# The end of a fused attention and feed-forward kernel: the last tile's operands turned by TensorE, products and results moved to GpSimd and ScalarE

## The chip, the cores and the metric

The kernel runs on one core of one Trainium2 chip. The metric is the device time of one execution in microseconds (us). Engines: TensorE (PE, with its weight load PEld), VectorE (DVE), ScalarE (ACT), GpSimd (POOL) and SyncE (SP), which only issues DMAs. Each engine works through its own instructions in the order in which the kernel writes them.

## The reference

`x` is 64 x 64 x 1024 in float32, 4096 tokens of 1024 numbers. The reference is

```
x = x + attn(cond(x))           # a 64x64 product per batch row, 32 heads, output projection
x = x + ffn(cond2(x))           # cond2: base product, plus a routed low-rank term
```

Only the second line's last part matters here. For a tile of 128 tokens, `z = cond2(x)` is rounded to bfloat16, and then

```
def dynamic_quant(x, inv):                       # per token
    xs = x * inv
    scale = max(max(abs(xs)) / 127, 1e-8)
    return clip(round(xs / scale), -127, 127), scale

qg, sg = dynamic_quant(z, inv_gate);  qu, su = dynamic_quant(z, inv_up)
gate = (qg @ w_gate.T) * sg * s_wgate            # 1024 -> 512
up   = (qu @ w_up.T)   * su * s_wup
inter = bfloat16(clip(silu(gate) * up, -10, 10))
qi, si = dynamic_quant(inter, inv_inter)         # 512 wide
out = x + (qi @ w_down.T) * si * s_wdown         # 512 -> 1024
```

## The kernel before

Tokens come in 32 tiles of 128, worked in 16 pairs. Attention fills the first two thirds of the time, then the output projection, then `second_stage`. There a software pipeline holds three pairs at once: a pair's router and base products run while the pair before it is in its quantized products and the one before that in its `down` products. The order of all steps is written out by hand (`manual_schedule`): first a loop over pairs, then a straight list of calls for the last three. In that list `p` is the last pair, `q` the one before it, `r` the one before that; (q, 1) below means tile 1 of pair q. So the order of the calls is the order on each engine, and a call that issues work on several engines takes a place in each of their queues.

The steps of one tile, with the names of their tiles and the lines of the profile:

- `rounded` (L1497): ScalarE rounds the base product out of PSUM to `z`.
- `quant_a` (L1531, L1535): VectorE multiplies `z` (or `inter`) by the inverse smoothing row into `q_g`, `q_u` or `q_i`, and takes the largest absolute value `am`. `quant_half` (L1546, L1547) and `quant_whole` (L1553) do the same by halves of 512 for the last tile, (p, 1), as its second half of `z` comes late.
- `scaled_down`: VectorE makes the scale `sc` (L1559) and its reciprocal `rs` (L1561), and ScalarE rounds in two activations (L1562, L1564) to `qb` in bfloat16.
- `quant_b`: VectorE clips `qb` (L1572), and the tile is transposed to `qT`, by a DMA from SP (L1575), or, with `by_pe`, by TensorE into PSUM (L1579, tile `qTp`) and a ScalarE copy (L1580). Only the `i` operands of the last pair go by TensorE.
- `gate_or_up` (L1589): eight matmuls give `pg` or `pu` in PSUM.
- `scaled` (L1594, L1600): VectorE scales into `og` or `ou` by a scalar_tensor_tensor (STT below); ScalarE takes the sigmoid `e` of `og`.
- `glu` (L1606, L1607, L1609): VectorE makes `inter`. It goes through `quant_a` and `quant_b` as `i`.
- `down` (L1619): two halves of four matmuls each give `pd` in PSUM.
- `result`: VectorE scales `pd` into `y` (L1628). For most tiles GpSimd then issues a DMA that adds `y` to the output in memory (L1636). For (q, 1) and the last pair, `x` is already on the chip (`x_l`, `x_ll`): GpSimd or VectorE adds it (L1632), and SP stores each half (L1633).

Tiles of the pool `p2` have two buffers for each tag, those of `p1p` one; a new tile waits until the old one in its buffer has no reader left, and a DMA that reads it counts. The tag of `y` is

```
y = p2.tile([P, H], F32, tag="q" if p == NPAIR - 1 else "y", name=f"y_{p}_{t}")
```

so that `y` of the last pair uses the buffers of `q_g` and `q_u`. Small products, and those of the last tile, share eight PSUM banks in two pools of four.

Of the kernel before, what the change touches and what calls it, by code (L numbers as in the profile page):

```python
# [11 lines left out]
F32 = mybir.dt.float32  # L12
# [3 lines left out]
AF = mybir.ActivationFunctionType  # L16
ALU = mybir.AluOpType
AX = mybir.AxisListType
PSUM = bass.MemoryType.PSUM

P = 128
# [1264 lines left out]
def second_stage(tc, a, out_t, xT_d, ident, ps_g, KC, NT, H, C, half, comb, op):  # L1286


    nc = tc.nc
# [7 lines left out]
    hs = [slice(0, HH), slice(HH, H)]  # L1297

    with ExitStack() as ctx:
# [7 lines left out]
        def load_row(name, src, n, pool=None):  # L1307
            t = (pool or w).tile([P, n], F32, tag=name, name=name)
            nc.sync.dma_start(t, bcast_rows(src))
            return t  # L1310
# [35 lines left out]
        p2 = ctx.enter_context(tc.tile_pool(name="q3", bufs=2, reuse_waits="tile"))  # L1346
# [3 lines left out]
        st = st1  # L1350
# [12 lines left out]
        sd_w = load_row("sd_w", a["s_wdown"], H)  # L1363
# [131 lines left out]
        def rounded(p, t, n):  # L1495
            s = st[p]
            nc.scalar.copy(s["z"][:, t, hs[n]], s.pop(("ps", t, n)))  # L1497
# [22 lines left out]
            elif i == 3:  # L1520
                nc.vector.tensor_tensor(z[:, 1, hs[0]], ps, s.pop("u2"), ALU.add)

        def quant_a(p, t, nm, between=None):

            s = st[p]
            src, inv, n = {
                "g": (lambda: s["z"][:, t, :], ig, H), "u": (lambda: s["z"][:, t, :], iu, H),
                "i": (lambda: s.pop(("inter", t)), ii, I),
            }[nm]
            q = p2.tile([P, n], F32, tag="q" + ("i" if nm == "i" else ""), name=f"q_{nm}_{p}_{t}")  # L1530
            nc.vector.tensor_tensor(q, src(), inv, ALU.mult)  # L1531
            if between:
                quant_b(*between)
            am = sm.tile([P, 1], F32, tag="am" + nm, name=f"am_{nm}_{p}_{t}")
            nc.vector.tensor_reduce(am, q, AX.X, ALU.max, apply_absolute_value=True)  # L1535
            scaled_down(p, t, nm, q, am, n)

        def quant_half(p, t, nm, n):

            s = st[p]  # L1540
            inv = ig if nm == "g" else iu
            if n == 0:
                s["q", nm] = p2.tile([P, H], F32, tag="q", name=f"q_{nm}_{p}_{t}")
                s["am", nm] = sm.tile([P, 2], F32, tag="amh" + nm, name=f"amh_{nm}_{p}_{t}")
            q = s["q", nm][:, hs[n]]
            nc.vector.tensor_tensor(q, s["z"][:, t, hs[n]], inv[:, hs[n]], ALU.mult)  # L1546
            nc.vector.tensor_reduce(s["am", nm][:, n:n + 1], q, AX.X, ALU.max, apply_absolute_value=True)  # L1547

        def quant_whole(p, t, nm):
            s = st[p]  # L1550
            q, am2 = s.pop(("q", nm)), s.pop(("am", nm))
            am = sm.tile([P, 1], F32, tag="am" + nm, name=f"am_{nm}_{p}_{t}")
            nc.vector.tensor_tensor(am, am2[:, 0:1], am2[:, 1:2], ALU.max)  # L1553
            scaled_down(p, t, nm, q, am, H)

        def scaled_down(p, t, nm, q, am, n):
            s = st[p]
            sc = s["sc", nm, t] = sm.tile([P, 1], F32, tag="sc" + nm, name=f"sc_{nm}_{p}_{t}", bufs=4)
            nc.vector.tensor_scalar(sc, am, 1.0 / QMAX, 1e-8, ALU.mult, ALU.max)  # L1559
            rs = sm.tile([P, 1], F32, tag="rs" + nm, name=f"rs_{nm}_{p}_{t}")  # L1560
            nc.vector.reciprocal(rs, sc)  # L1561
            nc.scalar.activation(q, q, AF.Copy, bias=MAGIC, scale=rs)  # L1562
            qb = s["qb", nm, t] = p2.tile([P, n], BF16, tag="qb" + nm, name=f"qb_{nm}_{p}_{t}")
            nc.scalar.activation(qb, q, AF.Copy, bias=-MAGIC)  # L1564

        def quant_b(p, t, nm, by_pe=False):


            s = st[p]
            n = I if nm == "i" else H  # L1570
            qb = s.pop(("qb", nm, t))
            nc.vector.tensor_scalar(qb, qb, QMAX, -QMAX, ALU.min, ALU.max)  # L1572
            s["qT", nm, t] = qT = p2.tile([P, n // P, P], BF16, tag="qT" + nm, name=f"qT_{nm}_{p}_{t}")
            if not by_pe:
                nc.sync.dma_start(qT, qb, transpose=True)  # L1575
                return
            ps = ps_g.tile([P, n // P, P], BF16, tag="g", name=f"qTp_{nm}_{p}_{t}")
            for c in range(n // P):
                nc.tensor.transpose(ps[:, c, :], qb[:, c * P:(c + 1) * P], ident_b)  # L1579
            nc.scalar.copy(qT, ps)  # L1580

        def gate_or_up(p, t, nm):
            s = st[p]
            qT = s.pop(("qT", nm, t))

            pool, tag = (ps_g, "g") if (p, t) == (NPAIR - 1, 1) else (ps_h, "h")
            ps = s["pgu", nm, t] = pool.tile([P, I], F32, tag=tag, name=f"p{nm}_{p}_{t}")
            for k in range(KC):
                nc.tensor.matmul(ps, qT[:, k, :], wt_b["w" + nm][:, k, :], start=(k == 0), stop=(k == KC - 1))  # L1589

        def scaled(p, t, nm):
            s = st[p]
            o = p1p.tile([P, I], F32, tag="o" + nm, name=f"o{nm}_{p}_{t}")
            nc.vector.scalar_tensor_tensor(  # L1594
                o, s.pop(("pgu", nm, t)), s.pop(("sc", nm, t)), sg_w if nm == "g" else su_w, ALU.mult, ALU.mult
            )
            s["o", nm, t] = o
            if nm == "g":
                e = p1p.tile([P, I], F32, tag="e", name=f"e_{p}_{t}")
                nc.scalar.activation(e, o, AF.Sigmoid)  # L1600
                s["e", t] = e

        def glu(p, t):
            s = st[p]
            e, g, u = s.pop(("e", t)), s.pop(("o", "g", t)), s.pop(("o", "u", t))
            nc.vector.tensor_mul(e, g, e)  # L1606
            nc.vector.tensor_mul(e, e, u)  # L1607
            inter = p1p.tile([P, I], BF16, tag="inter", name=f"inter_{p}_{t}")
            nc.vector.tensor_scalar(inter, e, LIMIT, -LIMIT, ALU.min, ALU.max)  # L1609
            s["inter", t] = inter  # L1610

        def down(p, t):
            s = st[p]
            qT = s.pop(("qT", "i", t))
            for n in range(2):
                pool, tag = (ps_g, "g") if p == NPAIR - 1 else (ps_h, "h")
                ps = s["pd", t, n] = pool.tile([P, HH], F32, tag=tag, name=f"pd_{p}_{t}_{n}")
                for k in range(IC):
                    nc.tensor.matmul(  # L1619
                        ps, qT[:, k, :], wt_b["wd"][:, k, hs[n]], start=(k == 0), stop=(k == IC - 1)  # L1620
                    )

        def result(p, t, *adds):
            s = st[p]
            y = p2.tile([P, H], F32, tag="q" if p == NPAIR - 1 else "y", name=f"y_{p}_{t}")
            si = s.pop(("sc", "i", t))
            for n in range(2):
                nc.vector.scalar_tensor_tensor(  # L1628
                    y[:, hs[n]], s.pop(("pd", t, n)), si, sd_w[:, hs[n]], ALU.mult, ALU.mult
                )  # L1630
                if adds:
                    adds[n % len(adds)].tensor_add(y[:, hs[n]], y[:, hs[n]], s["x", t][:, hs[n]])  # L1632
                    nc.sync.dma_start(out_t[2 * p + t, :, hs[n]], y[:, hs[n]])  # L1633
            if not adds:

                nc.gpsimd.dma_start(out_t[2 * p + t], y, accum_op=ALU.add)  # L1636

        def do(when, f, *args):
# [5 lines left out]
        for p in range(NPAIR - 1):  # L1644
            q, r = p - 1, p - 2
# [53 lines left out]
        p, q, r = NPAIR - 1, NPAIR - 2, NPAIR - 3  # L1699
# [14 lines left out]
        route(p)  # L1714
        quant_b(r, 1, "i")
        result(r, 0)
        quant_a(q, 0, "u")
        down(r, 1)
# [25 lines left out]
        glu(q, 1)  # L1744
        gate_or_up(p, 0, "g")
        rounded(p, 1, 1)
        quant_half(p, 1, "g", 0)
        quant_half(p, 1, "u", 0)
        gate_or_up(p, 0, "u")
        quant_half(p, 1, "g", 1)  # L1750
        quant_whole(p, 1, "g")
        quant_b(q, 0, "i")
        quant_half(p, 1, "u", 1)
        quant_whole(p, 1, "u")
        down(q, 0)
        quant_b(p, 1, "g")
        quant_a(q, 1, "i")
        scaled(p, 0, "g")
        scaled(p, 0, "u")
        quant_b(p, 1, "u")  # L1760
        gate_or_up(p, 1, "g")
        glu(p, 0)
        quant_b(q, 1, "i")
        gate_or_up(p, 1, "u")
        quant_a(p, 0, "i")
        scaled(p, 1, "g")
        scaled(p, 1, "u")
        down(q, 1)
        quant_b(p, 0, "i", True)
        glu(p, 1)  # L1770
        quant_a(p, 1, "i")
        result(q, 0)
        down(p, 0)
        quant_b(p, 1, "i", True)
        result(q, 1, nc.gpsimd)
        result(p, 0, nc.gpsimd, nc.vector)
        down(p, 1)
        result(p, 1, nc.vector)

# [53 lines left out]
```

## Time and profile before

| | before |
|---|---|
| median of 3 runs | 2405.47 us (2402.76 to 2409.4) |
| the profiled execution's own time | 2406.19 us |
| its span, first to last instruction | 2404.4 us |
| mean granted TensorE clock | 0.997 |
| TensorE busy | 2367.6 us (98%) |
| VectorE busy | 1334.5 us (56%) |
| ScalarE busy | 936.2 us (39%) |
| GpSimd busy | 418.7 us (17%) |
| last matmul of a base product (pb) starts | 2369.9 us |
| last instruction of VectorE ends | 2397.7 us |

All times inside the span count from its start. In the profile's rows a group is named by line, engine, operation, output and inputs, shape and count; a bracket gives the engine's idle time before it and what ended that. A wait is put down to the semaphore that came last. A busy TensorE is not TensorE at its peak, since matmuls overlap. In the windows each engine has its busy time and number of instructions, then the granted clock, the DMA engines' share and the rate.

### The profile page before, as it was taken

How to read it: one execution, taken by the hardware profiler on the slowest of the kernel's cores; microseconds unless marked ns; L12 is line 12 of the kernel's file. 1: busy time of each engine (PE TensorE's matmuls, PEld its weight loads, DVE VectorE, ACT ScalarE, POOL GpSimd, SP SyncE). 2: the span in 40 equal slices, each digit the busy share in tenths (PEclk: the TensorE clock that was granted, in tenths of full speed). 3: DMA queues.
4: the chain of work that ended last, by engine and by line, in shares of the span. 5: the costliest groups of instructions: out<-in, count | busy, mean ns of one | idle time of the engine just before them, and what ended most of it. 6: DMA issues, size and time to landing. Idle time of an engine off the chain costs nothing.

```text
span 2404.4 us, 41907 instructions
## 1 busy us (share of the span) xinstructions
PE 2367.6 (98%) x17066; PEld 1628.5 (68%) x17104; DVE 1334.5 (56%) x2584; ACT 936.2 (39%) x1220; POOL 418.7 (17%) x470
## 2 busy tenths in 40 slices
PE   8999999999999999999999999999999999999997
PEld 7888888888888888888888444444454545454452
DVE  3573474464543644633535533324377878777787
ACT  1344344343344443443434544343333333333333
POOL 4121112111122223220000333334100000000000
PEclk9999999999999999999999999999999999999999
DMA  7899799899899998997967788877733443444353
GB/s 229 217 240 248 190 228 241 221 232 220 208 232 274 212 255 230 242 237 179 207 188 196 213 257 258 275 218 248 239 77 75 90 79 83 84 86 82 70 119 76
DMA packets 612395, 453.84 MB, mean 189 GB/s; under 512 B 362465, under 2 KB 524258, under 8 KB 606690
## 3 DMA queue, kind: packets, MB, share of 16 engines
q1 hardware_dynamic: 581522, 393.91, 63.2%
q0 software_dynamic: 12240, 40.38, 7.9%
q10 hardware_dynamic: 18432, 16.79, 3.1%
q8 instruction: 137, 2.24, 0.4%
q14 instruction: 64, 0.52, 0.1%
HBM read 274.02 MB, written 91.23 MB: 152 GB/s over the span
## 4 chain that ended last, share of the span: by engine, by line
PE 92%; DMA 2%; DVE 1%; SPq 1%; issue 1%; ACT 0%; ACTq 0%; DVEq 0%
PE poa L1129 5%; PE poc L1129 5%; PE pod L1129 5%; PE psvc L530 4%; PE psva L530 4%; PE psvd L530 4%; PE pbc L1129 4%; PE pbd L1129 4%; PE pba L1129 4%; PE pskc L509 4%; PE pskd L509 4%; PE pska L509 4%; PE psqa L509 4%; PE psqd L509 4%; PE psqc L509 4%; PE pr L1398 2%
## 5 line engine op out<-in xcount | busy, mean ns | idle before, releaser
L582 ACT ACTIVATE prob<-prob 128x512 f32<-128x512 f32 x128 | 80.6, 629 | 346.7 <-DVE prob L578 338.6
L608 ACT COPY pT<-phT 128x1024 int16<-128x1024 int16 x128 | 165.4, 1339 | 25.4 <-DMA phT<-ph 21.4
L596 ACT COPY ph<-prob 128x1024 int16<-128x1024 int16 x128 | 133.5, 1043 | 63.1 <-DVE prob L590 38.4
L442 POOL COPY yB<-yhT 128x512 int16<-128x512 int16 (+1 forms) x84 | 75.8, 955 | 426.4 <-DMA yhT<-yh 426.4
L1636 POOL DMA_DIRECT2D out_dram<-y x29 | 25.2, 869 | 656.2 <-DVE y L1628 644.4
L577 DVE TENSOR_REDUCE mx<-s 128x8 f32<-128x512 f32 x128 | 87.4, 682 | 71.6 <-PE s L568 71.6
L1250 POOL TENSOR_TENSOR xo<-xo,ob 128x1024 f32<-128x1024 f32 x32 | 83.5, 2629 | 228.2 <-DVE prob L578 189.5
L509 PE MATMUL psqa<-yB,wq 128*128 128x256 f32 x512 | 121.1, 379 | 0.5 <-ACT psqp L479 0.5
L509 PE MATMUL pska<-yB,wk 128*128 128x256 f32 x512 | 120.9, 379 | 0.0
L1224 ACT COPY xh<-xo 128x1024 int16<-128x1024 int16 x64 | 64.4, 1041 | 142.8 <-DVE xo L1269 142.8
L530 PE MATMUL psva<-wv,yB 128*128 128x256 f32 x512 | 115.8, 379 | 0.0
L1129 PE MATMUL poa<-woA,cx 128*128 128x512 f32 x256 | 115.3, 593 | 0.0
L1129 PE MATMUL pba<-wtA,x1T 128*128 128x512 f32 x240 | 107.9, 592 | 0.0
L1235 ACT COPY xTo<-xhT 128x1024 int16<-128x1024 int16 x64 | 84.7, 1337 | 58.4 <-DMA xhT<-xh 53.3
L530 PEld LDWEIGHTS psva<-wv,yB 128*128 128x128 f32 x512 | 97.2, 190 | 14.0 <-issue 0.8
L509 PEld LDWEIGHTS psqa<-yB,wq 128*128 128x128 f32 x512 | 97.1, 190 | 14.0 <-ACT psqp L479 0.9
L509 PEld LDWEIGHTS pska<-yB,wk 128*128 128x128 f32 x512 | 97.3, 190 | 13.2
L633 ACT ACTIVATE co<-banks,bqkv 128x256 f32<-128x256 f32 x128 | 60.7, 474 | 109.3 <-PE banks L411 79.8
L1266 POOL TENSOR_TENSOR xo<-xo,ou 128x512 f32<-128x512 f32 x48 | 59.9, 1275 | 191.8 <-DVE ou L1263 191.8
L590 DVE TENSOR_TENSOR prob<-prob,den 128x512 f32<-128x512 f32 x128 | 89.4, 699 | 4.4
L578 DVE TENSOR_TENSOR prob<-s,mx 128x512 f32<-128x512 f32 x128 | 88.5, 691 | 4.5
L1129 PEld LDWEIGHTS poa<-woA,cx 128*128 128x128 f32 x256 | 48.5, 190 | 60.0 <-issue 59.5
(255 smaller groups left out, 4945.8 us busy)
## 6 DMA issues: line engine op xcount, KB each, us to landing
wv<-v_d SPq DMA_DIRECT2D x56, 512.0 KB
wq<-q_d SPq DMA_DIRECT2D x28, 1024.0 KB
wk<-k_d SPq DMA_DIRECT2D x28, 1024.0 KB
wq<-in_qkvw_dram SPq DMA_DIRECT2D x100, 256.0 KB
wk<-in_qkvw_dram SPq DMA_DIRECT2D x100, 256.0 KB
wv<-in_qkvw_dram SPq DMA_DIRECT2D x50, 512.0 KB
x<-in_x_dram SPq DMA_DIRECT2D x32, 512.0 KB
ctx_d<-co ACTq DMA_DIRECT2D x128, 128.0 KB
```

The costliest lines, as they stand in the source:

```text
L442: nc.gpsimd.tensor_copy(dst, src[:, :, :, halves[r] if hf else r])
L509: nc.tensor.matmul(ps[:, 0:HB], A[:, SLOT[A_OF[i]], k, :], B[B_OF[i]][:, k, :], start=first and k == 0, stop=k == KQ - 1, skip_group_check ...
L530: nc.tensor.matmul(ps[:, j * VC:(j + 1) * VC], B[B_OF[i]][:, k, j * P:(j + 1) * P], A[:, k, :], start=first and j == 0 and k == 0, stop=k ...
L577: nc.vector.tensor_reduce(mx, ps[:, :, n, :, :], AX.X, ALU.max)
L578: nc.vector.tensor_tensor(p.rearrange("p j h k -> p h j k"), ps[:, :, n, :, :], mx.unsqueeze(3).to_broadcast([P, HPC, 2, C]), ALU.subtract,)
L582: nc.scalar.activation(p, p, AF.Exp, scale=scale)
L590: nc.vector.tensor_tensor(p, p, den.unsqueeze(2).to_broadcast([P, n, C]), ALU.mult)
L596: nc.scalar.copy(h, planes(p.rearrange("p n k -> p (n k)")))
L608: nc.scalar.copy(planes(pT.rearrange("p a b q -> p (a b q)")), hT)
L1129: self.nc.tensor.matmul(ps, self.B[self.B_OF[i]][:, k, :], self.A[self.A_OF[i]][:, k, :], start=first and k == 0, stop=k == self.KQ - 1, s ...
L1235: nc.scalar.copy(planes(xT.rearrange("p k q -> p (k q)")), hT)
L1250: nc.gpsimd.tensor_add(s["x"][:, t, :], s["x"][:, t, :], self.ob)
```

## The change

It is made in the helpers of the end and in the order of the last calls.

- `quant_b` has no yes or no any more but takes the function that copies the transposed operand out of PSUM. The gate operand of (p, 1) is turned by TensorE and copied by VectorE, its up operand turned by TensorE and copied by ScalarE; before, DMAs turned both.
- `quant_a` and `quant_half` take the engine of the product. GpSimd does the second half of `q_u` of (p, 1), and `q_i` of (q, 1) and of (p, 0). The maximum of a half is a step of its own (`half_maximum`).
- `result_by_act` does the results of pair q: ScalarE scales `pd` by the token's scale, GpSimd multiplies by the row `sd_w`, and for (q, 1) GpSimd also adds `x`. Its `y` has the tag `q`.
- The order: the clip and DMA of `qb_i` of (q, 0) come after both scales of (p, 1); `result` of (q, 0) moves up ahead of `glu(p, 0)`; `result` of (p, 0) moves ahead of the last tile's `quant_b`.

```diff
-        def quant_half(p, t, nm, n):
+        def quant_half(p, t, nm, n, eng=nc.vector):
...
-            nc.vector.tensor_tensor(q, s["z"][:, t, hs[n]], inv[:, hs[n]], ALU.mult)
-            nc.vector.tensor_reduce(s["am", nm][:, n:n + 1], q, AX.X, ALU.max, apply_absolute_value=True)
+            eng.tensor_tensor(q, s["z"][:, t, hs[n]], inv[:, hs[n]], ALU.mult)
+            s["am2", nm, n] = lambda: nc.vector.tensor_reduce(
+                s["am", nm][:, n:n + 1], q, AX.X, ALU.max, apply_absolute_value=True
+            )
+
+        def half_maximum(p, nm, n):
+            st[p].pop(("am2", nm, n))()
...
-        def quant_b(p, t, nm, by_pe=False):
+        def quant_b(p, t, nm, by_pe=None):
...
-            nc.scalar.copy(qT, ps)
+            by_pe(qT, ps)
...
+        def result_by_act(p, t, add):
+
+            s = st[p]
+            y = p2.tile([P, H], F32, tag="q", name=f"y_{p}_{t}")
+            si = s.pop(("sc", "i", t))
+            for n in range(2):
+                nc.scalar.activation(y[:, hs[n]], s.pop(("pd", t, n)), AF.Copy, scale=si)
+                nc.gpsimd.tensor_tensor(y[:, hs[n]], y[:, hs[n]], sd_w[:, hs[n]], ALU.mult)
+                if add:
+                    nc.gpsimd.tensor_add(y[:, hs[n]], y[:, hs[n]], s["x", t][:, hs[n]])
+                    nc.sync.dma_start(out_t[2 * p + t, :, hs[n]], y[:, hs[n]])
+            if not add:
+                nc.gpsimd.dma_start(out_t[2 * p + t], y, accum_op=ALU.add)
...
-        quant_half(p, 1, "g", 0)
-        quant_half(p, 1, "u", 0)
+        for nm in ("g", "u"):
+            quant_half(p, 1, nm, 0)
+            half_maximum(p, nm, 0)
         gate_or_up(p, 0, "u")
+        quant_half(p, 1, "u", 1, nc.gpsimd)
         quant_half(p, 1, "g", 1)
+        half_maximum(p, "g", 1)
         quant_whole(p, 1, "g")
+        half_maximum(p, "u", 1)
+        quant_whole(p, 1, "u")
         quant_b(q, 0, "i")
-        quant_half(p, 1, "u", 1)
-        quant_whole(p, 1, "u")
+        quant_a(q, 1, "i", None, nc.gpsimd)
         down(q, 0)
-        quant_b(p, 1, "g")
-        quant_a(q, 1, "i")
         scaled(p, 0, "g")
+        quant_b(p, 1, "g", nc.vector.tensor_copy)
         scaled(p, 0, "u")
-        quant_b(p, 1, "u")
+        quant_b(p, 1, "u", nc.scalar.copy)
         gate_or_up(p, 1, "g")
+        result_by_act(q, 0, False)
+        quant_b(q, 1, "i")
         glu(p, 0)
-        quant_b(q, 1, "i")
         gate_or_up(p, 1, "u")
-        quant_a(p, 0, "i")
+        quant_a(p, 0, "i", None, nc.gpsimd)
         scaled(p, 1, "g")
         scaled(p, 1, "u")
         down(q, 1)
-        quant_b(p, 0, "i", True)
         glu(p, 1)
+        quant_b(p, 0, "i", nc.scalar.copy)
+        result_by_act(q, 1, True)
         quant_a(p, 1, "i")
-        result(q, 0)
         down(p, 0)
-        quant_b(p, 1, "i", True)
-        result(q, 1, nc.gpsimd)
         result(p, 0, nc.gpsimd, nc.vector)
+        quant_b(p, 1, "i", nc.scalar.copy)
         down(p, 1)
         result(p, 1, nc.vector)
```

More of the change, by code (lines that the diff above doesn't have):

```diff
@@ L1521, in after, with quant_a @@
                 nc.vector.tensor_tensor(z[:, 1, hs[0]], ps, s.pop("u2"), ALU.add)
-        def quant_a(p, t, nm, between=None):
+        def quant_a(p, t, nm, between=None, eng=nc.vector):
             s = st[p]
@@ L1530, in quant_a @@
             q = p2.tile([P, n], F32, tag="q" + ("i" if nm == "i" else ""), name=f"q_{nm}_{p}_{t}")
-            nc.vector.tensor_tensor(q, src(), inv, ALU.mult)
+            eng.tensor_tensor(q, src(), inv, ALU.mult)
             if between:
```

## The prediction

> **What bounds the kernel now.** I read the page first, then the windows of the end, the chain of waits there, the timeline of the last 30 us, and last the rows that price what is new.
>
> ```profile
> PE 2367.6 (98%) x17066; PEld 1628.5 (68%) x17104; DVE 1334.5 (56%) x2584; ACT 936.2 (39%) x1220; POOL 418.7 (17%) x470
> ```
> ```profile
> core 0: us, PE busy (x) PEld busy (x) DVE busy (x) ACT busy (x) POOL busy (x), PEclk, DMA share, GB/s
> 2328.00:2371.00 43.00, 42.84 (x132) 19.72 (x134) 32.84 (x71) 17.62 (x23) 1.72 (x2) 1.00 0.42 89
> 2371.00:2383.00 12.00, 7.29 (x33) 2.84 (x32) 10.77 (x25) 6.33 (x8) 0.00 (x0) 1.00 0.30 56
> 2383.00:2405.00 22.00, 8.29 (x38) 3.28 (x37) 13.78 (x24) 4.40 (x7) 5.03 (x4) 0.72 0.40 105
> ```
>
> TensorE is full up to 2371 us and nothing ahead of that is edited, so the change lives in the last 33 us. There VectorE is the busy engine (10.77 of 12 us), GpSimd is empty until 2390. The chain of waits (start, us, what):
>
> ```profile
> 2375.49 0.43 DVE qb_g L1572
> ...
> 2379.33 3.12 DMA qT_u<-qb_u
> 2382.46 0.05 issue
> 2382.50 1.92 PE pu L1589 x8
> ...
> 2390.72 2.73 DVE y L1628 x4
> ...
> 2397.02 0.69 DVE y L1632
> ```
>
> The end is a row of small steps of the last tile (p,1), one transposing DMA of 3.1 us on it, and, after its last clip at 2390.51, VectorE works off eight result steps until 2397.71. From there to the span's end, 6.7 us of stores and closing work are left as they are.
>
> Now the prices. The timeline, and one line's instructions with GpSimd beside it (To) and without (T):
>
> ```profile
> 2390.66 0.86 POOL L1636 DMA_DIRECT2D out_dram<-y  x1 [41.66 <-DVE y L1628]
> 2391.61 2.50 POOL L1632 TENSOR_TENSOR y<-y,x_l 128x512 f32<-128x512 f32 x2
> 2393.48 1.18 DVE L1632 TENSOR_TENSOR y<-y,x_ll 128x512 f32<-128x512 f32 x1
> 2394.07 1.71 POOL L1632 TENSOR_TENSOR y<-y,x_ll 128x512 f32<-128x512 f32 x1
> ```
> ```profile
> L1142 DVE TENSOR_TENSOR To<-cx,To x16: 678/2832/2839, 1325.0 to 1680.8; 128x512 f32<-128x512 f32 x16
> L1142 DVE TENSOR_TENSOR T<-x1T,T x15: 680/683/687, 1716.0 to 2288.0; 128x512 f32<-128x512 f32 x15
> ```
>
> A 512-wide product costs GpSimd 1.26 us against VectorE's 0.69, a store issued by GpSimd holds its queue for 0.86, and GpSimd runs strictly one after the other. A VectorE step with two operands in SBUF that meets a GpSimd product waits until that ends (1.18; 2.83 for 0.68), and GpSimd waits likewise (1.71, ending 1.12 after VectorE's). Steps that read PSUM (L1628, 0.68 each at 2390.72) do not wait. The clock, by windows:
>
> ```profile
> 658.75:662.16 3.41, 1.25 (x6) 1.16 (x7) 0.29 (x1) 3.38 (x4) 0.00 (x0) 1.00 0.79 168
> 662.20:665.50 3.30, 3.30 (x10) 2.59 (x9) 1.89 (x4) 0.32 (x1) 2.15 (x5) 0.50 1.16 312
> 2389.30:2392.70 3.40, 1.16 (x8) 0.63 (x9) 3.25 (x7) 1.73 (x3) 1.95 (x2) 1.00 0.33 23
> 2392.70:2397.70 5.00, 2.11 (x6) 0.46 (x3) 4.90 (x7) 0.00 (x0) 3.08 (x3) 0.50 0.91 245
> ```
>
> Stretches of 3.4 us with TensorE 37% and 34% busy are followed by half the clock.
>
> **The change part by part.** I lay the new written order on each engine with the durations above; between engines 0.04 us pass, 0.14 into GpSimd, and VectorE's next step starts 0.03 after the last one's end if it needs it, 0.08 before it if not, all as the timeline of before shows.
>
> *The second half of q_u to GpSimd, clip of (q,0) moved back.* [...] The clip of qb_i(q,0) stood right behind rs_g (2373.10); now the u maximum (0.69) and am, sc, rs (0.19 each, 0.2 of waiting for GpSimd's q_i(q,1)) go first: 2374.55 to 2374.84. Its DMA needs 2.46 as before (2373.40 to 2375.86), so down(q,0) starts at 2377.33, not 2375.86.
>
> *The last tile's operands turned by TensorE.* Removed: two DMAs of 3.1 us each and their two issues (1.23 each) on SP, which holds nothing else up. Added: eight transposes (row of qTp_i: four in 0.40, 0.056 apart, so 0.61) and a copy of 1024 out of PSUM each. ScalarE copies 1024 16-bit elements out of PSUM in 1.01 (L420). VectorE's copy has no row: 0.42 (the 1024 clip) to 1.23 (the 1024 product); I take 1.22, as for one element a step. By itself a turn of about 1.75 for 3.1. But the transposes of qb_g stand behind down(q,0) on TensorE: 2377.33 + 8 x 0.216 = 2379.06, though qb_g is clipped at 2376.83. They end at 2379.67, and VectorE, whose next instruction is the copy, stands idle for 2.9 us with ou, the u clip, the clip of (q,1) and glu(p,0) queued behind it. Copy to 2380.92, ou 0.74 and clip 0.42 to 2381.92, u transposes to 2382.59, ScalarE's copy to 2383.64. The DMA delivered u at 2382.50: the 1.3 us that a turn saves are gone.
>
> *The results of (q,0) and the product of (p,0).* ScalarE's first half of y (0.59, the PSUM copy, to 0.72, the scaled activation; 0.68 taken) follows that copy: 2384.23. Then GpSimd's queue: 0.14, two products 2.49 (2386.86), the store's issue 0.14 + 0.86 (2387.86), and only then q_i(p,0), to 2389.09. VectorE had that product at 2382.27. Nothing covers the difference: VectorE's next instruction is the maximum of that product, and og, ou and glu of (p,1) queue behind it, though pg is there at 2384.3. **+6.8 us.** Products with a bf16 operand have no GpSimd row: 0.61 (its cast) to 1.71; 1.26 taken.
>
> *From there to rs of (p,1).* Maximum, sc, rs 1.11 (2390.20); og, ou to 2391.51; sigmoid behind ScalarE's q_i, qb_i to 2392.15; glu 1.91 (2394.06); clip of (p,0), product, maximum, sc, rs to 2395.97. That is 6.9 us against 6.8 in before (2382.27 to 2389.06): no change.
>
> *The last steps.* Taken off VectorE: four result steps of 0.68, 2.7 us. But result(p,0) is moved ahead of the last clip and waits for down(p,0), which starts at 2395.70 and, after 6 us without work for TensorE, at half clock (0.43 a matmul, as at 2392.9) ends at 2399.35: STT 2400.13, add 2400.85 (at full clock 2.1 less for the STT, 1.6 for the add, which then meets GpSimd). ScalarE's y(q,1) delays q_i(p,1) by 0.7, hidden by that. Clip of (p,1): 2401.05, up to 1.1 more beside a GpSimd product (no row shows a clip there: 0 to 1.26). Transposes, copy and down at half clock, with that 1.1: the halves lie ready near 2405.5 and 2407.2. There is a new wait too: y of q now uses the buffers named q, so y(p,1) may be written only when y(q,1) is stored. GpSimd's four steps on it (2396.37 plus 4 x 1.26, 0.3 and 0.2 of waits) end at 2401.97; a store from SP needs 0 to 5.5 (the accumulating store's landing), and I take 3.4, since traffic goes on that long after the last issue at 2398.27: 2405.4. Then 0.74 + 0.69 + 0.74 + 0.69: the last add ends at 2408.2 (full clock) to 2408.7, against 2397.71. From rs of (p,1) that is 12.2 to 12.7 us against 8.65 in before (2389.06 to 2397.71), +3.6 to +4.1. **Sum:** 6.8 + 0.1 + 4.1 = **+11.0**, taken at half clock, which the idle stretch ahead is nearest to; +10.5 at full clock.
>
> *The clock.* TensorE waits 3.3 us in one piece (2374.0 to 2377.33), less busy over most cuts into 3.4 us than the two stretches that were halved. Then down(q,0) takes up to 1.73 more, on the path: 0 to +1.75. [...]
>
> [...]
>
> **The rivals.** *TensorE's turning is what counts (faster).* Place: VectorE's queue. It is rid of three products and four result steps (2.7 us), the chain of the DMA in it (3.1 for 1.75). Price: -2.7 and -1.3, near 2401.5. Point: it decides if q_i(p,0) leaves GpSimd by 2382.3, so ScalarE's first half of y by 2377.4, when down(q,0) has just begun. For: GpSimd is empty there in before. Against: the written order.
> *GpSimd's queue does not bind (within 0.3%).* Should q_i(p,0) not have to wait for y(q,0) and its store, it is done near 2385.3 (inter at 2383.92, 0.14, 1.26) instead of 2389.1, the tail follows 3.8 earlier, and y(q,1) is stored in time for y(p,1), 0.5 more: +6.7, near 2412. Point: q_i(p,0) done before y(q,0)'s first product. For: inter is ready 0.45 before that product starts. Against: the queue is served in the written order, as all of before's timeline shows.
> *The clock falls early as well (slower still).* +11.0 and, as the cut falls, half to all of the 1.75: near 2418.
>
> **How the numbers follow.** The profiled execution took 2406.19 for a span of 2404.4; the runs' median of 2405.47 is 0.72 below it. 2406.19 + 11.0 - 0.72 = 2416.5. Chances: forecast 0.63, early clock 0.20, queue that does not bind 0.11, faster 0.06. Low end: copy at 0.42 (-0.8), bf16 product at 0.61 (-0.65), shorter store wait (-0.5) and most of the second rival (-4.3): 2411. High end: the early clock, 1.75, and a store wait of 5.5 in place of 3.4: 2420. 0.3% is 7.2 us, about what a measurement of this kernel can tell from no change; only the second rival lies within it, only the first is faster.
>
> **What would show it.** Right: VectorE idle for some 2.9 us before a PSUM copy at 2379.7; the maximum of (p,0) waiting on POOL until 2389; down(p,1) or the first y of (p,1) past 2403, with 0.50 in the clock. Wrong: q_i(p,0) on POOL before 2385, transposes of qb_g before 2378, or a last add before 2404.

## The result and the profile after

| | before | after |
|---|---|---|
| median, 12 runs each | 2402.27 us (2398.86 to 2409.4) | 2415.45 us (2409.31 to 2419.88) |
| ratio of the runs | | 1.0048, interval [1.0038, 1.0058] |
| profiled execution, span | 2406.19, 2404.4 us | 2414.44, 2412.6 us |
| last `z` row (L1497) ends | 2371.16 | 2368.52 |
| from there to VectorE's last addition | 26.56 | 38.36 |
| from there to the end of the span | 33.23 | 44.11 |

The changed kernel is slower by 0.48% of 2402 us, 11.5 us (9.1 to 13.9); the two medians lie 13.2 us apart. In the profiles the section behind the last `z` row is 10.9 us longer, against +11.0 in the forecast's sum. What lies ahead of that row isn't edited, yet its end falls anywhere from 2364.0 to 2372.1 us in the profiles below. So the traces are compared from that row on, and a time "after z" counts from it.

Line numbers behind `half_maximum` have moved by five (the `quant_b` clip is L1577, the PSUM copy L1585, `down` L1624, the result STT L1633, and `result_by_act` is L1649 to L1655). The page's line of busy time and the windows of the end (us, busy time of each engine, granted clock, DMA share, GB/s):

```profile
PE 2373.7 (98%) x17120; PEld 1628.5 (67%) x17120; DVE 1334.2 (55%) x2578; ACT 940.0 (39%) x1225; POOL 426.5 (18%) x477
```
```profile
2328.00:2368.50 40.50, 40.50 (x119) 18.13 (x118) 30.45 (x63) 16.95 (x22) 1.72 (x2) 1.00 0.38 69
2368.50:2380.50 12.00, 7.08 (x34) 3.08 (x32) 7.06 (x20) 6.08 (x8) 2.79 (x2) 0.86 0.06 11
2380.50:2400.50 20.00, 9.82 (x45) 3.92 (x42) 11.05 (x20) 7.04 (x11) 10.23 (x9) 0.70 0.24 46
```

The busy sums hardly differ. In the first 12 us after z VectorE was busy for 10.77 before and is for 7.06 now: it was relieved, and it waits. GpSimd's 10.23 us in the 20 us behind that are twice the 5.03 that it had in before's last 22 us. The chain of waits says for what (start, us, what):

```profile
2374.50 3.41 PE pd L1624 x8
...
2382.64 0.56 POOL y L1650
...
2385.43 0.88 POOL out_dram L1655
2386.30 1.20 POOL q_i L1531
2387.53 0.70 DVE am_i L1535
...
2394.05 3.61 PE pd L1624 x8
...
2397.69 0.76 DVE y L1633
...
2399.08 1.36 DVE qb_i L1577
...
2401.77 3.61 PE pd L1624 x8
2405.41 0.76 DVE y L1633
2406.19 0.69 DVE y L1637
```

The y of (q,0), its store and then `q_i` of (p,0) follow each other on GpSimd, as forecast, and all of it is on the chain. Three `down` at half clock (3.41, and 3.61 for each tile of the last pair) and a clip of 1.36 are there as well. The timeline, with the idle time ahead of an instruction and what ended it:

```profile
2378.57 0.69 DVE L1585 COPY qT_g<-qTp_g 128x1024 bf16<-128x1024 bf16 x1 [4.58 <-PE qTp_g L1584]
2386.00 1.49 POOL L1531 TENSOR_TENSOR q_i<-inter,ii 128x512 f32<-128x512 bf16 x1
2387.53 0.69 DVE L1535 TENSOR_REDUCE am_i<-q_i 128x1 f32<-128x512 f32 x1 [5.29 <-POOL q_i L1531]
2399.08 1.35 DVE L1577 TENSOR_SCALAR qb_i<-qb_i 128x512 bf16<-128x512 bf16 x1
2403.76 0.75 DVE L1633 SCALAR_TENSOR_TENSOR y<-pd,sc_i,sd_w 128x512 f32<-128x512 f32 x1 [3.33 <-PE pd L1624]
```

Two stops of VectorE, 4.58 us for the transposes and 5.29 us for GpSimd's product, add up to more than the loss up to `rs` of (p,1), 7.98 us; VectorE was rid of three products of 0.68 us there. The last line's releaser matters too: the first y of (p,1) waited for TensorE and not for a store. The clock, by windows cut where it changed:

```profile
2371.25:2374.70 3.45, 0.30 (x2) 0.11 (x2) 2.56 (x10) 3.39 (x4) 0.14 (x1) 1.00 0.20 38
2374.75:2378.10 3.35, 3.35 (x12) 1.42 (x11) 0.00 (x0) 2.07 (x4) 0.00 (x0) 0.50 0.00 0
2385.00:2388.40 3.40, 1.10 (x6) 0.29 (x3) 0.84 (x2) 0.00 (x0) 2.19 (x3) 1.00 0.52 60
2388.45:2405.40 16.95, 8.41 (x24) 2.77 (x24) 9.97 (x17) 5.45 (x9) 6.73 (x5) 0.50 0.27 83
```

TensorE's wait for the late operand of down(q,0) (0.30 us busy in 3.45) was followed by half the clock just as down(q,0) began, and 32% of busy time in the third window did not prevent the second fall. Whether the clock falls over the first wait is not fixed by the steps up to it. Five profiles have the same steps and the same wait: in the kernel after and the first three experiments below it fell 6.2, 6.4, 7.2 and 7.1 us after z, and in the last experiment of the next section not before 18.0. So part of what separates single profiles below is where the clock fell.

### The profile page after: what moved, and what is told of

Read it like the earlier page. It is cut to its first block, busy times and chain, and to the rows that moved or that the text cites. A ratio compares the mean times of both kernels' runs of the same rounds, so it can differ in the third digit from the quotient of the medians.

```text
span 2412.6 us, 41982 instructions
## 1 busy us (share of the span) xinstructions
PE 2373.7 (98%) x17120; PEld 1628.5 (67%) x17120; DVE 1334.2 (55%) x2578; ACT 940.0 (39%) x1225; POOL 426.5 (18%) x477
## 4 chain that ended last, share of the span: by engine, by line
PE 92%; DVE 1%; DMA 1%; SPq 1%; issue 0%; ACT 0%; POOL 0%; ACTq 0%; DVEq 0%
PE poa L1129 5%; PE pod L1129 5%; PE poc L1129 5%; PE psvc L530 4%; PE psva L530 4%; PE psvd L530 4%; PE pbc L1129 4%; PE pba L1129 4%; PE pbd L1129 4%; PE pskd L509 4%; PE pskc L509 4%; PE pska L509 4%; PE psqa L509 4%; PE psqd L509 4%; PE psqc L509 4%; PE pr L1398 2%
## 5 line engine op out<-in xcount | busy, mean ns | idle before, releaser
L509 PEld LDWEIGHTS pska<-yB,wk 128*128 128x128 f32 x512 | 97.3, 190 | 13.2
```

The source lines that it names most:

```text
L509: nc.tensor.matmul(ps[:, 0:HB], A[:, SLOT[A_OF[i]], k, :], B[B_OF[i]][:, k, :], start=first and k == 0, stop=k == KQ - 1, skip_group_check ...
```

## Experiments on the kernel after

The theory: the product of (p,0) stands behind y of (q,0) and its store in GpSimd's queue, and that is most of the loss; the late operand of down(q,0), the clock and the last section make the rest. Its rivals: the turning by TensorE itself, the shared buffers of y, GpSimd's work as such.

**The product ahead of y(q,0).**

```diff
-        result_by_act(q, 0, False)
         quant_b(q, 1, "i")
         glu(p, 0)
         gate_or_up(p, 1, "u")
         quant_a(p, 0, "i", None, nc.gpsimd)
+        result_by_act(q, 0, False)
```

> The changed kernel with one call moved: GpSimd's product q_i of (p,0) is issued ahead of the results of (q,0), so it no longer stands behind two products and a store. The tail, from the end of the last z row to the end of VectorE's last add, is 26.6 us in the kernel before and 38.4 in the changed one; q_i of (p,0) ends 19.0 after z. Theory (the order of GpSimd's queue holds VectorE): the product ends 13.6 to 15.4 after z, some 3.8 sooner, and the rows up to rs of (p,1) follow at least 1.5 sooner; the whole tail shortens less, 35.4 to 37.1, since the results of (q,0) then run beside later steps. Rival (the clock and the late down(q,0) set the tail): the product ends sooner but rs of (p,1) stays where it is and the tail stays within 0.5 of 38.4. [...]

Measured: 2411.49 us, ratio to before 1.0034 [1.0020, 1.0049]; last addition 37.87 after z (38.36 in the kernel after). The product itself was done 4.0 us sooner (14.96 after z for 18.97), `rs` of (p,1) only 1.7 sooner (24.16 for 25.89), and of the sum 0.5 remained. The timeline shows three places where the gain went:

```profile
2378.57 1.16 POOL L1531 TENSOR_TENSOR q_i<-inter,ii 128x512 f32<-128x512 bf16 x1 [10.92 <-DVE inter L1614]
2382.97 2.94 POOL L1650 TENSOR_TENSOR y<-y,sd_w 128x512 f32<-128x512 f32 x2 [3.24 <-ACT y L1649]
2384.82 1.63 DVE L1612 TENSOR_TENSOR e<-e,ou 128x512 f32<-128x512 f32 x1
2391.71 1.41 DVE L1633 SCALAR_TENSOR_TENSOR y<-pd,sc_i,sd_w 128x512 f32<-128x512 f32 x2 [2.76 <-DMA out_dram<-y]
```

y(q,0) now stands on ScalarE ahead of the sigmoid of (p,1), its GpSimd products hold the second step of glu(p,1) (1.63 for 0.69), and its later store holds the buffer that y(p,0) needs: VectorE waited 2.76 us for that DMA to land. The wait was moved, not removed. Of the expectation the product and `rs` came as the theory had them; the section, 35.4 to 37.1 expected, did not.

**The product back on VectorE.**

```diff
-        quant_a(p, 0, "i", None, nc.gpsimd)
+        quant_a(p, 0, "i")
```

> The changed kernel with the one product q_i of (p,0) back on VectorE, all else as changed. Theory (GpSimd's queue is the largest term, 6.8 us in the prediction, and part of it comes back later): q_i of (p,0) ends 13.0 to 14.7 after z for 19.0, rs of (p,1) 4.3 sooner, the tail 31.9 to 33.7 us for 38.4, the time 4.5 to 6 us shorter. Rival (the clock and the late down(q,0)): the tail changes by under 1 us. What is left above before's 26.6, 5 to 7 us, is then the late down(q,0), its clock, and the results ahead of the last clip.

Measured: 2408.25 us, ratio 1.0015 [1.0004, 1.0026]; last addition 32.87 after z, span's end 39.95 after z. One argument of one call takes 5.5 us off the section up to the last addition, and 4.2 up to the end of the span. `q_i` of (p,0) ends 13.71 after z, 5.3 sooner. 0.7 of that is the clock, which fell later in this profile (transposes of `qb_g` end 9.29 after z for 10.01). In the profile of after, `inter` of (p,0) was ready 13.71 after z, and a product on VectorE behind it would have ended near 14.4 (an estimate with the 0.72 us from `inter` to the product's end in this run). So of the 7.9 us by which the product was late there, GpSimd's queue made about 4.5, and the late down(q,0), its half clock and the turning behind it 3.3. The section came as expected; the whole time fell by more than the 4.5 to 6 us, by 7.2 between the medians.

**y of pair q in buffers of its own.**

```diff
-            y = p2.tile([P, H], F32, tag="q", name=f"y_{p}_{t}")
+            y = p2.tile([P, H], F32, tag="y", name=f"y_{p}_{t}")
```

> The changed kernel with y of pair q in buffers of its own (tag y) in place of those named q, so that y of (p,1) need not wait until y of (q,1) is stored. Theory (the store is one of two things that end near together): the tail 37.3 to 38.4 us for 38.4, at most 1.1 less, and VectorE's first STT of (p,1) then waits for TensorE. Rival (the buffers set the end): the tail falls by 2 us or more.

Measured in one run: 2411.5 us; last addition 38.13, end 44.38 after z (38.36 and 44.11 with shared buffers), and from `rs` of (p,1) to the last addition 12.48 us for 12.47. The shared buffers cost nothing that these two profiles can tell apart, in agreement with the releaser of the last y above.

**TensorE kept busy over its wait for down(q,0).** 14 more matmuls into a PSUM tile that nobody reads.

```diff
+        busy = ps_g.tile([P, HH], F32, tag="g", name="busy")
+        for _ in range(14):
+            nc.tensor.matmul(busy, ident_b, wt_b["wg"][:, 0, :], start=True, stop=True)
         quant_half(p, 1, "u", 1, nc.gpsimd)
```

> The changed kernel with 14 extra matmuls into an unread PSUM tile behind pu of (p,0), 3.0 us of work in TensorE's wait for down(q,0), so that no stretch of 3.4 us there is nearly empty; they add work and no result. Theory (the early half clock cost the path 1.3 us in the changed kernel's trace): the granted clock stays at 1.00 there, down(q,0) takes 1.9 us for 3.4, the transposes of qb_g end 8.0 to 8.6 after z for 10.0, and the tail is 36.7 to 37.6 us for 38.4. Rival (the clock is no part of it): no change of the tail, 38.0 to 38.8.

```profile
2368.13 3.19 PE L1772 MATMUL busy<-wg,ident_b 128*128 128x512 bf16 x14
2371.45 1.90 PE L1624 MATMUL pd<-wd,qT_i 128*128 128x512 bf16 x8
```

Measured in one run: 2409.53 us; last addition 36.34, end 42.27 after z. The clock stayed at 1.00 until 20.9 after z, down(q,0) took 1.90 for 3.41, the transposes of `qb_g` ended 8.34 after z for 10.01, and the section is 1.8 to 2.0 us shorter. So a profile without the early fall is about 2 us shorter than that of after, slightly more than was expected. That the extra matmuls prevented the fall is not shown by this one run: in the profile of the three mends, next, it stayed away without them.

**Three mends at once:** the product on VectorE, y of pair q in its own buffers, and the clip of (p,1) ahead of the results of (p,0).

```diff
-            y = p2.tile([P, H], F32, tag="q", name=f"y_{p}_{t}")
+            y = p2.tile([P, H], F32, tag="y", name=f"y_{p}_{t}")
...
-        quant_a(p, 0, "i", None, nc.gpsimd)
+        quant_a(p, 0, "i")
...
-        result(p, 0, nc.gpsimd, nc.vector)
         quant_b(p, 1, "i", nc.scalar.copy)
+        result(p, 0, nc.gpsimd, nc.vector)
```

> The kernel after with three edits: q_i(p,0) on VectorE, the y of (q,0) and (q,1) in buffers of their own, and the clip and turning of (p,1) issued ahead of the results of (p,0). Measure: from the end of the last z row to the end of the last addition, 26.56 us before, 38.36 after, 32.87 with the product alone on VectorE. If the clip beside GpSimd (1.35 for 0.29) and the results that stand ahead of it are the rest of the loss in the last section: 28.9 to 30.7, the clip at 0.25 to 0.35, and 2 to 4 us less time than with the product alone on VectorE. If the last section is long for another cause (ScalarE's and GpSimd's work on (q,1)): 32 to 34 still.

```profile
2377.58 1.90 PE L1624 MATMUL pd<-wd,qT_i 128*128 128x512 bf16 x8 [3.15 <-DMA qT_i<-qb_i]
...
2392.83 1.27 POOL L1652 TENSOR_TENSOR y<-y,x_l 128x512 f32<-128x512 f32 x1
2393.28 0.96 DVE L1577 TENSOR_SCALAR qb_i<-qb_i 128x512 bf16<-128x512 bf16 x1 [2.05 <-ACT qb_i L1569]
```

Measured: last addition 29.10, end 35.41 after z, 3.8 and 4.5 us below the kernel with the product alone on VectorE. 1.4 of the 3.8 lie ahead of `rs` of (p,1), where down(q,0) ran at the full clock (1.90 for 2.44). Behind it, from `rs` to the last addition, it is 9.46 us for 11.82: as own buffers for y changed nothing before, this is what the clip ahead of the results of (p,0) is worth. The clip still met a GpSimd addition, that of (q,1), and took 0.96, not 0.3. The times don't show the step: 2409.39 us, ratio 1.0023 [1.0008, 1.0037], against 1.0015 [1.0004, 1.0026] with the product alone. The clock also fell at other places in the two profiles (here first 18.0 after z, there 7.2), and one profile of each can't part all of that from the edits. Of the expectation the sum held, the clip and the time did not.

## Experiments on the kernel before: each part alone

**Only the turning.** `quant_b(p, 1, "g", nc.vector.tensor_copy)` and `quant_b(p, 1, "u", nc.scalar.copy)` in before's order.

```diff
-        quant_b(p, 1, "g")
+        quant_b(p, 1, "g", nc.vector.tensor_copy)
...
-        quant_b(p, 1, "u")
+        quant_b(p, 1, "u", nc.scalar.copy)
```

> Before's call order, with the last tile's two operands turned by TensorE (g copied by VectorE, u by ScalarE) and nothing else changed. Measure: from the end of the last z row to the end of the last addition, 26.56 us in the kernel before and 38.36 in the one after. If the turning itself costs: the g operand's transposes stand behind down(q,0) on TensorE and VectorE, in order, waits for them before q_i(q,1); 30.0 to 31.0, q_i(p,0) ending about 14.2 after z instead of 11.1, time +3 to +4.5 us. If only GpSimd's queue costs (the prediction's 6.8) and the turning is free (its 0.1 here): 26.4 to 27.2, time within 1 us of before.

```profile
2371.48 1.90 PE L1619 MATMUL pd<-wd,qT_i 128*128 128x512 bf16 x8 [1.87 <-DMA qT_i<-qb_i]
2373.22 0.61 PE L1579 MATMUL qTp_g<-ident_b,qb_g 128*128 128x128 bf16 x8
2373.87 0.69 DVE L1580 COPY qT_g<-qTp_g 128x1024 bf16<-128x1024 bf16 x1 [2.33 <-PE qTp_g L1579]
```

Measured: 2405.53 us, ratio 1.0012 [1.0002, 1.0021]; last addition 30.90, `q_i` of (p,0) 14.13 after z, both as expected for a turning that costs. A faster turn (0.61 + 0.69 for a DMA of 3.1) makes the kernel slower, since its transposes stand behind down(q,0) and VectorE waits 2.33 us in its own queue for them: `q_i` of (p,0) is 3.0 late. The other 1.3 us came with TensorE's half clock (from 9.3 after z; the gate product of (p,1) took 3.62 for 1.90). The DMA needed neither queue.

**Only the results of pair q** through ScalarE and GpSimd, at before's places, in the tag `y`.

```diff
-        result(q, 0)
+        result_by_act(q, 0, False)
         down(p, 0)
         quant_b(p, 1, "i", True)
-        result(q, 1, nc.gpsimd)
+        result_by_act(q, 1, True)
```

> Before's call order, with the results of (q,0) and (q,1) through ScalarE and GpSimd, in buffers of their own, at their places of before (after the quantization of (p,1)). If the moved results harm only through what is queued behind them (nothing here), VectorE is relieved of four operations: 25.6 to 26.5, up to 1 us less than before's 26.56. If operations of GpSimd beside VectorE's last ones cost of themselves: the clip of (p,1) at 1.35 instead of 0.285 and the last section longer, 27 to 29.

```profile
2387.96 2.38 DVE L1632 TENSOR_TENSOR y<-y,x_ll 128x512 f32<-128x512 f32 x1
2388.19 1.59 POOL L1645 TENSOR_TENSOR y<-y,sd_w 128x512 f32<-128x512 f32 x1
...
2393.21 1.26 POOL L1647 TENSOR_TENSOR y<-y,x_l 128x512 f32<-128x512 f32 x1
2394.43 1.26 POOL L1632 TENSOR_TENSOR y<-y,x_ll 128x512 f32<-128x512 f32 x1
```

Measured: 2407.72 us, ratio 1.0029 [1.0018, 1.0040]; VectorE's last addition 27.62 after z, but GpSimd's 31.30, and the span ends 38.54 after z for 33.23. Neither expectation had that. 27.62 lies in the range of the second, but the end is another engine's: GpSimd, with seven 512-wide steps and a store in its queue, becomes the engine that ends last. And the clip, which that expectation put at 1.35, took its usual 0.29; a VectorE addition took 2.38 for 0.69.

**Only the three products** on GpSimd.

```diff
+        quant_half(p, 1, "u", 1, nc.gpsimd)
         quant_half(p, 1, "g", 1)
+        half_maximum(p, "g", 1)
...
-        quant_half(p, 1, "u", 1)
+        half_maximum(p, "u", 1)
...
-        quant_a(q, 1, "i")
+        quant_a(q, 1, "i", None, nc.gpsimd)
...
-        quant_a(p, 0, "i")
+        quant_a(p, 0, "i", None, nc.gpsimd)
```

> Before's call order, with only the three products (q_u second half, q_i(q,1), q_i(p,0)) on GpSimd. Nothing else is in GpSimd's queue at that time. If a product there costs only its longer run (1.49 for 0.69) and what VectorE waits for it: 27.0 to 27.8, +0.5 to +1.2 us. If GpSimd is harmful whatever stands ahead: three times some 0.8 to 1.8 in line, 29 to 32.

Measured: 2403.44 us, ratio 1.0003 [0.9994, 1.0013]; last addition 26.96, end 33.23 after z. With nothing ahead of it in GpSimd's queue, the product of (p,0) starts at once and costs 0.4 us. The same line costs about 4.5 in the full change (5.5 with the clock's part): its price lies in what is queued ahead of it. The clip of (q,0) was held beside GpSimd here (0.96 us for 0.27), and the clock fell early too (5.0 after z, down(q,0) 3.29 us); no transposes stand behind down(q,0) in this kernel, and the section hardly felt it.

**Only the order** of calls, every operation on its engine of before. The edit takes the engine arguments out of after's list:

```diff
-        quant_half(p, 1, "u", 1, nc.gpsimd)
+        quant_half(p, 1, "u", 1)
...
-        quant_a(q, 1, "i", None, nc.gpsimd)
+        quant_a(q, 1, "i")
...
-        quant_b(p, 1, "g", nc.vector.tensor_copy)
+        quant_b(p, 1, "g")
         scaled(p, 0, "u")
-        quant_b(p, 1, "u", nc.scalar.copy)
+        quant_b(p, 1, "u")
...
-        result_by_act(q, 0, False)
+        result(q, 0)
...
-        quant_a(p, 0, "i", None, nc.gpsimd)
+        quant_a(p, 0, "i")
...
-        result_by_act(q, 1, True)
+        result(q, 1, nc.gpsimd)
```

> The kernel after's call order with every operation left on the engine that it had before: products on VectorE, the last tile's operands turned by DMA, results of (q,0) and (q,1) by VectorE (with (q,1)'s addition on GpSimd). The prediction priced the order almost at nothing outside of the moved engines. If that holds: 26.5 to 27.5. If the order itself costs (VectorE's results of (q,0) stand ahead of glu(p,0) and wait for down(q,0), whose operand is clipped later; the last results of (p,0) stand ahead of the clip of (p,1)): 28.6 to 31.6, q_i(p,0) ending 12 to 13.7 after z, time +2 to +5 us.

```profile
2376.55 0.75 DVE L1633 SCALAR_TENSOR_TENSOR y<-pd,sc_i,sd_w 128x512 f32<-128x512 f32 x1 [0.73 <-PE pd L1624]
2378.26 0.75 DVE L1633 SCALAR_TENSOR_TENSOR y<-pd,sc_i,sd_w 128x512 f32<-128x512 f32 x1 [0.95 <-PE pd L1624]
```

Measured: 2407.0 us, ratio 1.0013 [1.0003, 1.0023]; last addition 31.21, end 36.60 after z. The order alone costs some 3 us: y(q,0), moved up, stops VectorE's queue twice (0.73 and 0.95) for the later down(q,0), and the clock fell early here too (5.4 after z). From `rs` of (p,1) to the last addition it is 8.75 us, as in before (8.65): results of (p,0) ahead of the clip cost nothing here, where down(p,0) starts 2.4 us ahead of `rs`; in the kernel after it starts only 0.4 ahead. The prediction did charge this part of the order, in its last steps.

The four parts alone make +4.6, +5.3, 0.0 and +3.4 us at the span's end in one profile each, 13.3 together, against 10.9 for the whole. They overlap, and the part that is free by itself is dear in company: of the three products, the one of (p,0) alone gave back 4.2.

## Experiments towards a version that beats both

The parts left one candidate: relieve VectorE of the result of (q,0) only.

```diff
+        result_by_act(q, 0, False)
         quant_a(p, 1, "i")
-        result(q, 0)
+        result(q, 1, nc.gpsimd)
         down(p, 0)
         quant_b(p, 1, "i", True)
-        result(q, 1, nc.gpsimd)
```

> Before's kernel with one thing of the change: the result of (q,0) through ScalarE and GpSimd, in a buffer of its own, issued after glu(p,1), and the result of (q,1) as before but issued ahead of down(p,0). With both results moved, GpSimd's last addition ended 3.7 us after VectorE's and set the end. If one result of the two is what GpSimd can take there: last addition 25.3 to 26.3 after z (before 26.56), GpSimd's last one earlier than VectorE's, time 0 to 1 us below before. If two-input operations of VectorE beside GpSimd cost more than the two that are saved: 27 to 28.5, 0.5 to 2 us more.

Measured: 2405.98 us, ratio 1.0008 [0.9995, 1.0021]; last addition 27.41, end 33.24 after z, so the second expectation. The timeline shows what took the gain: GpSimd's last addition did end earlier than VectorE's, but an addition of VectorE was held for 3.62 us beside three of GpSimd.

```profile
2386.10 2.81 POOL L1632 TENSOR_TENSOR y<-y,x_l 128x512 f32<-128x512 f32 x2
2387.06 3.62 DVE L1632 TENSOR_TENSOR y<-y,x_ll 128x512 f32<-128x512 f32 x1
2388.55 1.58 POOL L1632 TENSOR_TENSOR y<-y,x_ll 128x512 f32<-128x512 f32 x1
```

The same with an order made for it:

```diff
         quant_half(p, 1, "g", 1)
+        quant_half(p, 1, "u", 1)
+        half_maximum(p, "g", 1)
         quant_whole(p, 1, "g")
         quant_b(q, 0, "i")
-        quant_half(p, 1, "u", 1)
+        half_maximum(p, "u", 1)
+        scaled(p, 0, "u")
         quant_whole(p, 1, "u")
-        down(q, 0)
+        scaled(p, 0, "g")
         quant_b(p, 1, "g")
         quant_a(q, 1, "i")
-        scaled(p, 0, "g")
-        scaled(p, 0, "u")
+        down(q, 0)
         quant_b(p, 1, "u")
-        gate_or_up(p, 1, "g")
         glu(p, 0)
         quant_b(q, 1, "i")
+        gate_or_up(p, 1, "g")
...
         glu(p, 1)
-        quant_a(p, 1, "i")
-        result(q, 0)
         down(p, 0)
-        quant_b(p, 1, "i", True)
+        result_by_act(q, 0, False)
+        quant_a(p, 1, "i")
         result(q, 1, nc.gpsimd)
+        quant_b(p, 1, "i", True)
```

> The same one result moved, in an order of calls that was chosen for it: (p,0)'s two scaled rows ahead of the clip of g, down(p,0) ahead of the result of (q,0), the result of (q,1) ahead of the clip of (p,1). No product on GpSimd, no turning of (p,1)'s operands by TensorE. Worked out from the durations of the traces so far: last addition 24.5 to 25.5 after z (before 26.56), time 1 to 2 us below before, which is less than 0.1%. If contention with GpSimd takes it back: 26.5 to 28, time as before or up to 1.5 us more.

```profile
2391.43 2.82 POOL L1638 TENSOR_TENSOR y<-y,x_l 128x512 f32<-128x512 f32 x2
2392.39 3.63 DVE L1638 TENSOR_TENSOR y<-y,x_ll 128x512 f32<-128x512 f32 x1
2393.88 1.58 POOL L1638 TENSOR_TENSOR y<-y,x_ll 128x512 f32<-128x512 f32 x1
```

Measured: 2407.39 us, ratio 1.0014 [1.0002, 1.0025]; last addition 26.69, end 32.27 after z. Up to the last section the order gains (`q_i` of (p,1) ends 16.08 after z for 16.80 before), and then one addition of VectorE is held for 3.63 us, through three GpSimd additions in a row. The section fits the expectation of contention; the time, 3.4 us more (0.5 to 6.0), is above both. The test of the hold:

```diff
-        result(q, 1, nc.gpsimd)
+        result(q, 1)
...
-        result(p, 0, nc.gpsimd, nc.vector)
+        result(p, 0, nc.vector)
```

> The kernel of the run before (one result of (q,0) through ScalarE and GpSimd, its own order of calls), with the additions taken off GpSimd: the result of (q,1) goes out through the accumulating store, as (q,0)'s does, and both additions of (p,0) are VectorE's. There VectorE's one addition of (p,0) lasted 3.63 us while GpSimd ran three additions beside it, against 0.69 alone, and the last addition ended 26.69 after z. If that hold is what took the gain back: the additions at 0.69 each, the last one 24.2 to 25.2 after z, the span ending 29.8 to 31.3 after z instead of 32.27 (33.23 before). If it was a wait for the stores, or the second accumulating store ends last: 26 to 27.5, the span ending 32 to 34. The whole time moves by at most 3 us, 0.1%, either way.

```profile
2388.11 1.19 POOL L1642 DMA_DIRECT2D out_dram<-y  x1
2388.41 0.69 DVE L1638 TENSOR_TENSOR y<-y,x_ll 128x512 f32<-128x512 f32 x1
...
2389.79 0.69 DVE L1638 TENSOR_TENSOR y<-y,x_ll 128x512 f32<-128x512 f32 x1
```

Measured: 2404.68 us, ratio 1.0006 [0.9997, 1.0014]; last addition 26.30, end 36.12 after z. Without GpSimd's additions beside them those of VectorE take 0.69 each, and from `q_i` of (p,1) to the last addition it is 8.39 us for 10.61. But the clock fell 6.3 after z, `q_i` of (p,1) was 1.8 later, and the accumulating store issued at 2388.11 took 9.3 us to land. The last addition lies in the range of the second expectation, the end above both. The hold is shown, the gain is not. No version beats the kernel before.

## Why the prediction was right, point by point

The forecast was 2416.5, range 2411 to 2420; the runs gave 2415.45, or +11.5 us by the ratio where the sum said +11.0. That the two times lie within 1.1 us is in part luck. The forecast stood on 2405.47 us, a median of three runs of before; twelve runs gave 2402.27, and from there the sum would have said 2413.3. And within the sum, an early fall of the clock, which its main case left out, was made up for by two other errors. In us after z, the sum's steps beside the trace (the forecast's times less before's 2371.16):

| step | forecast | after | before |
|---|---|---|---|
| down(q,0) starts | 6.17 | 5.98 | 4.71 |
| transposes of `qb_g` end | 8.51 | 10.01 | |
| VectorE's copy of it ends | 9.76 | 10.73 | |
| `qT_u` is there | 12.48 | 13.45 | 11.34 |
| `q_i` of (p,0) ends | 17.93 | 18.97 | 11.11 |
| `rs` of (p,1) | 24.81 | 25.89 | 17.91 |
| last addition | 37.0 to 37.5 | 38.36 | 26.56 |
| end of the span | 43.7 to 44.2 | 44.11 | 33.23 |

- **Late clip and down(q,0): right**, within 0.2 us. The sum's times hold 0.2 us there for `am_g` of (p,1) waiting for GpSimd's half of `q_u`. That was the author's estimate and no run shows it at that size: in the kernel after `am_g` took 0.28 us for 0.16 in before, 0.12 more.
- **The clock.** The forecast's sum left out an early fall and gave it a case of its own, 0 to +1.75, at a chance of 0.20. It came in this profile: down(q,0) at half clock put the transposes 1.50 late, and the profile with TensorE kept busy, where the clock did not fall, is 1.8 to 2.0 us shorter. It came in four of the five profiles that have this wait unfilled; that the wait would cost nothing was the author's estimate for the sum, and one profile of five shows it. The wait was 9% busy (0.30 us of 3.45); the clock fell as well behind the stretch that was 32% busy (1.10 of 3.40), and in before's rows behind 37% and 34%.
- **VectorE's copy out of PSUM: mis-sized**, 1.22 taken, 0.69 measured. It hid 0.53 of the clock's 1.50. Of its own range, 0.42 to 1.23, the prediction took the upper end; the middle was nearer. It moved 1024 elements in the 0.69 us that a 512-wide product took too; that it would need as long for each element as a product was the author's estimate, and no row showed it.
- **GpSimd's queue: right in mechanism.** Two products 1.26 each, 0.30 to the store, its issue 0.88, then the product. +6.8 was forecast for `q_i` of (p,0) and +7.9 came. The term was named after one cause but holds two. By the forecast's own times (`inter` ready at 2383.92) the late turn makes about 2.4 of it and the queue 4.4; measured, the late turn with its half clock made 3.3 and the queue about 4.5. The queue was sized right, and the excess is the clock's.
- **From there to `rs` of (p,1): right**, 6.92 us for 6.88.
- **The last steps: right in size**, 12.47 us from `rs` of (p,1) to the last addition, 12.2 to 12.7 forecast. The clip beside GpSimd took 1.35 for 0.28, a wait that no row of before had shown; the prediction put up to 1.1 on it, an estimate from the length of a GpSimd product (1.26). That results of (p,0) ahead of the clip are dear is borne out by the three mends: 2.4 us less behind `rs` with the clip ahead. The new buffer wait did not bind: at half clock the halves of down(p,1) released the last results, as one branch of the sum had it, and buffers of their own changed nothing that two profiles can tell.
- **The closing work** was taken as unchanged; it was 0.92 us shorter (5.75 for 6.67). This and the copy are what balanced the early clock: up to the last addition the trace was 0.9 to 1.4 us behind the forecast, at the span's end level with it.
- **The rivals.** "TensorE's turning is what counts" fell: the turning alone costs. "GpSimd's queue does not bind" did not happen, and its price of -4.3 was wrong: the product 4.0 earlier moved the end by only 0.5, since other steps of y(q,0) then stood in the way. "The clock falls early as well" did happen, but not its price of near 2418, for the reason above.
- **The 0.3%.** The prediction took 7.2 us as about what a measurement can tell from no change, and only its second rival as lying within that. The runs tell it finer, to 2.4 us on either side, and the first rival's 2401.5, 4 us below before, lies within 7.2 us too.

What stays open: why the whole times of the last kernels (1.0006 to 1.0023) don't follow the order of their end sections. Where the last `z` row ends scatters by 8 us, and one profile each does not say whether that differs by kernel.

## What to carry to other kernels

Before an operation goes to an idle engine, list what its new queue holds ahead of it at that place in the written order, and what of the old engine waits for it: the same product cost 0.4 us in an empty queue and about 4.5 behind a result and its store. A faster step that needs two busy queues can lose to a slower DMA that needs none: with the turn alone, 0.61 and 0.69 us for a DMA of 3.1, the last addition came 4.3 us later. Near the end of a kernel, don't put two-operand VectorE steps beside GpSimd work (one addition took 3.63 us for 0.69), and count with it that a wait of TensorE can cost more than its length: behind the one of 3.15 us here the clock fell to half in four profiles of five, and in the kernel after `down` of (q,0) then took 3.41 us for the 1.90 of the profile with TensorE kept busy.

## What the hardware did that was not expected

- A VectorE addition with both operands in SBUF was not let in between GpSimd's instructions: it was held through three in a row, 3.63 us for 0.69, ending 0.56 after the last of them, and 3.62 us in a second kernel.
- A clip with one operand in SBUF was held as well: 1.35 us in the kernel after and 0.96 in two others for 0.28, ending 0.15 us after GpSimd's instruction.
- A store that GpSimd issues landed 5.3 us after its issue in the kernel after (5.5 in before); the second of two that were issued back to back, 9.3 us after its issue.
